# Attention's side work: full-width expert products, the inverse root on GpSimd, and a wider step limit for VectorE

## The chip, the cores and the metric

The kernel runs on one core of a Trainium2 chip. The metric is the device time of one execution in microseconds. A core has TensorE (PE, with its weight loads listed as PEld), VectorE (DVE), ScalarE (ACT), GpSimd (POOL) and SyncE (SP), which here only issues transfers. Each engine works off its own queue in order and waits on semaphores of the others.

## The reference, cut to what matters

Input is x of 8 images, 128 channels, 64 x 64 pixels, in float32. Layer 0 is a Mamba-like scan block with group norm. Layer 1 sees each image as 4096 tokens of 128 channels and adds an additive attention and a mixture of 64 experts:

```python
t = _to_tokens(x)
t = t + _L1_attn_ref(_ln_t(t), W1, b1, w2, b2)          # causal: weights exp(w2 . tanh(f_i + g_j + b1) + b2)
t = t + _L1_ffn_ref(_ln_t(t), gate_w, gate_b, weight1, weight2)

def _ln_t(v, eps=1e-5):                                  # layer norm over the channels
    return (v - mean) / sqrt(var + eps)

# in _L1_ffn_ref, for each image and each of 64 experts:
probs = softmax(logits over the tokens)                  # logits = x @ gate_w.T + gate_b
vals, idx = top_k(probs, 8)                              # each expert takes its 8 best tokens
pooled = sum over the 8 of vals * x[idx]                 # a 128-vector for each expert
# ... two small dense layers on pooled; the result, times vals, is added back to those 8 tokens
```

The change lies in two places of this: in the layer norm before the experts (the factor 1/sqrt(var + eps)) and in the product that makes `pooled`.

## The kernel before, in words

The kernel has two large stages. `mamba` works through 64 chunks of 512 tokens (the first 1.5 ms). `attend` then works through the causal attention of all eight images, and at its end the experts' dense layers and the output.

**The attention loop.** The score matrix of an image is cut into tiles of 128 keys by 512 queries; the diagonal ones are packed, so that there are 132 tiles for each image and 1056 in all. The loop `for i in range(-3, n + 3)` is a software pipeline over them. For each `i` it issues, in this order:

- `rounds` (L718): PE makes the numerators N of tile i and the denominators D of tile i+3, as products with 32 rows of weights, four of them side by side in the array. D and N have one set of PSUM banks each.
- `logarithms` (L728, L729): ACT takes the logarithm of D into a tile called `mix`, which frees D.
- `inverses` (L735): ACT takes one exponential over four planes of 512 columns: three inverse denominators and the weights exp(-score) of an earlier tile.
- `ratios` (L740): DVE multiplies N by the inverses, three operations of 128 x 512; each frees a bank of N.
- `weigh` (L766): PE multiplies the finished weights of tile i-3 with the tokens and adds into the bank `av`. At the end of a row of tiles `take` (L777) copies `av` to `sums` on DVE.
- `advance(("p", "next", "alone"), ...)`: side steps that issue PE work (below).
- `causal` (L746): a mask on GpSimd, for diagonal tiles.
- `advance(("v", "free", "end"), ...)`: side steps for DVE.
- `scores` (L753, L754): DVE adds two of the ratios, GpSimd adds the third (128 x 512 each) into the plane that `inverses` exponentiates next.

**The side steps.** What follows the attention (its normalisation, the second layer norm, the logits, the choice of eight tokens, the product for `pooled`) is written as generators in two lanes, `finishing` and `routing`. Each `yield` names a kind and a written cost for what comes next: "p" opens a group of PE work in the one PSUM bank `ms`, "next" goes on with it, "free" is the DVE step that empties the bank, "v" is DVE work, and "end" ends the lane's turn in this tile. `advance` takes steps from the lanes' fronts as long as their kinds fit and their written costs stay within a limit (the first step is always taken):

```python
if spent and spent + cost > room or kind in ("p", "alone") and holder:
    break
```

The limit for PE is 0.37 (0.6 in the last image while `more` holds). For DVE it is 1.4 while `more` holds, that is, while more than three generators are listed in the two lanes, and otherwise 0.8.

For each of the 64 groups of 512 tokens, `finish` normalises the attention's result (L842 on PE, L847 to L851 on DVE), then `route` runs `normalise` (L792 bn_stats, L795 bn_aggr, L796 adding epsilon into `rs`, L798 and L799 on ACT for the inverse root, L802 four scalings into `lnf`), transposes (L811, L813) and makes logits (L878, L887, L889). Once for each image `choose` picks the tokens (L931 to L979, with ACT's exponentials in L944), and for seven of the eight images goes through four groups of: transposing the weights (L1007, L1010) and the product for `pooled` (L1016 on PE, L1026 or L1028 on DVE).

**The product.** A column of 128 weights holds 64 experts for a token block of the first half and the same 64 experts for a block of the second half. L1016 multiplies each 64-column half with its own block of 128 tokens, into its own 64 partitions of the bank. In the records each float32 product counts as two MATMULs.

Of the kernel before, what the change touches and what calls it, by code (L numbers as in the profile page):

```python
# [10 lines left out]
AF = mybir.ActivationFunctionType  # L11
ALU = mybir.AluOpType
AX = mybir.AxisListType

P = 128
# [3 lines left out]
NE = 64  # L19
# [43 lines left out]
def fast_path(  # L63
# [24 lines left out]
    nc = tc.nc  # L88
# [4 lines left out]
    NQ = CH // P  # L93
# [9 lines left out]
    def fixed(name, *shape):  # L103
        return const.tile(list(shape), F32, name=name)
# [10 lines left out]
    gamma, beta, gateb = fixed("gamma", P, 1), fixed("beta", P, 1), fixed("gateb", P, 1)  # L115
    wuv, biasv, wcol = fixed("wuv", P, 2, P), fixed("biasv", P, 1), fixed("wcol", P, 1)
    back, shift, tiny = fixed("back", P, P + 1), fixed("shift", P, 1), fixed("tiny", P, 1)
    floor = fixed("floor", P, 1)
    gwide = fixed("gwide", P, 3 * NE)

    def halves(queue, t, src):
# [2 lines left out]
    def prepare(mw, bank):  # L124
# [90 lines left out]
        nc.vector.tensor_scalar(tiny, tiny, 1e-10, None, ALU.mult)  # L215
        nc.vector.memset(shift, -SHIFT)
        nc.vector.memset(floor, EPS)
        nc.vector.tensor_reduce(gsel, ident.rearrange("p (g c) -> p g c", c=GROUP), AX.X, ALU.add)
        nc.vector.tensor_scalar(
            gmean3, gsel.unsqueeze(2).to_broadcast([P, P // GROUP, GROUP]), 1.0 / GROUP, None, ALU.mult  # L220
# [437 lines left out]
    def attend(aw, small, ap, remaining):  # L658
# [18 lines left out]
        n = len(tiles)  # L677
        per, held = n // B, []
        U, V, tok, tt, lnf = {}, {}, {}, {}, {}
# [101 lines left out]
        def bank(name):  # L781
            return ap.tile([P, CH], F32, tag="ms", name=name)

        def normalise(n, src, dst):

            st = small.tile([P, NQ, 6], F32, tag="st", name=f"st{n}")
            mv = small.tile([P, NQ, 2], F32, tag="lmv", name=f"lmv{n}")
            rs = small.tile([P, NQ], F32, tag="rs", name=f"rs{n}")
            for q in range(NQ):
                if q:  # L790
                    yield "v", 0.2
                nc.vector.bn_stats(st[:, q, :], src[:, q, :])  # L792
            yield "v", 0.45
            for q in range(NQ):
                nc.vector.bn_aggr(mv[:, q, :], st[:, q, :])  # L795
            nc.vector.tensor_scalar(rs, mv[:, :, 1], EPS, None, ALU.add)  # L796
            yield "end", 0.0
            nc.scalar.activation(rs, rs, AF.Ln)  # L798
            nc.scalar.activation(rs, rs, AF.Exp, scale=-0.5)  # L799
            for q in range(NQ):  # L800
                yield "v", 0.26
                nc.vector.tensor_scalar(  # L802
                    dst[:, q, :], src[:, q, :], mv[:, q, 0:1], rs[:, q : q + 1], ALU.subtract, ALU.mult
                )
# [10 lines left out]
        def bring(b, g):  # L815


            n = f"{b}_{g}"
            c = b * NCH + g
            u = U[b, g] = aw.tile([P, 2, CH], F32, tag="U", bufs=4, name=f"U{n}")  # L820
            v = V[b, g] = aw.tile([P, 2, CH], F32, tag="V", bufs=NCH + 1, name=f"V{n}")
            queue = nc.gpsimd if c < 3 else nc.sync
            for ab, to, at in ((0, 0, 64), (0, 64, 0), (1, 0, 96), (1, 64, 32)):
                for which in range(2):
                    rows = slice(to + 32 * which, to + 32 * (which + 1))
                    queue.dma_start(u[rows, ab, :], uv_dram[c][0, at : at + 32, :])
                    queue.dma_start(v[rows, ab, :], uv_dram[c][1 + which, at : at + 32, :])
            t = tt[b, g] = aw.tile([P, NQ, P], F32, tag="tt", bufs=NCH, name=f"tt{n}")
            k = tok[b, g] = aw.tile([P, NQ, P], F32, tag="tok", bufs=NCH + 1, name=f"tok{n}")
            for r, dst in enumerate((t, k)):  # L830
                nc.sync.dma_start(dst.rearrange("p q c -> p (q c)"), k_dram[c][r])
# [59 lines left out]
        def choose(b):  # L891

            n = f"{b}"
# [86 lines left out]
            if final:  # L980
# [3 lines left out]
                for g, tag in enumerate(("D2", "N0", "av", "ms")):  # L984
# [4 lines left out]
                    mT = aw.tile([P, NQ, P], F32, tag="mT", bufs=2, name=f"mT{n}_{g}")  # L989
# [5 lines left out]
                acc = aw.tile([P, P], F32, tag="acc", name=f"acc{n}")  # L995
                nc.vector.tensor_copy(acc, total)
                pp = ap.tile([P, CH], F32, tag="N0", name=f"pp{n}")
# [4 lines left out]
            for g in range(NCH // 2):  # L1002
                for q in range(NQ):
                    yield "next" if q else "p", 0.14
                    if q == 0:
                        pm = bank(f"pm{n}_{g}").rearrange("p (q e) -> p q e", e=P)
                    nc.tensor.transpose(pm[:, q, :], w[:, 2 * g + q // 2, ts(q % 2, P)], ident)  # L1007
                yield "free", 0.6
                mT = aw.tile([P, NQ, P], F32, tag="mT", bufs=2, name=f"mT{n}_{g}")
                nc.vector.tensor_copy(mT, pm)  # L1010
                for q in range(NQ):
                    yield "next" if q else "p", 0.18
                    if q == 0:
                        pp = bank(f"pp{n}_{g}")
                    for h in range(2):
                        nc.tensor.matmul(  # L1016
                            pp[ts(h, NE), :P],
                            lhsT=mT[:, q, ts(h, NE)],
                            rhs=lnf[b, 2 * g + q // 2][:, 2 * h + q % 2, :],
                            start=q == 0,  # L1020
                            stop=q == NQ - 1,
                        )
                yield "free", 0.3
                if g == 0:
                    acc = aw.tile([P, P], F32, tag="acc", name=f"acc{n}")
                    nc.vector.tensor_copy(acc, pp[:, :P])  # L1026
                else:
                    nc.vector.tensor_tensor(acc, acc, pp[:, :P], ALU.add)  # L1028
            yield "p", 0.26
            pp = bank(f"pp{n}")  # L1030
            nc.tensor.matmul(pp[:, :NE], lhsT=acc, rhs=stack, start=True, stop=True)
# [46 lines left out]
        def biases():  # L1078

            wb1 = aw.tile([NE, NH * P], F32, tag="wb1", name="wb1")  # L1080
            nc.sync.dma_start(wb1, weight1[:, P, :])
            wb2 = aw.tile([NE, P], F32, tag="wb2", name="wb2")
            nc.sync.dma_start(wb2, weight2[:, NH * P, :])
            return wb1, wb2
# [231 lines left out]
        def upcoming(lane):  # L1316

            while lane:
                if id(lane[0]) not in waits:
                    waits[id(lane[0])] = next(lane[0], None)  # L1320
                if waits[id(lane[0])] is not None:
                    return waits[id(lane[0])]
                del waits[id(lane[0])]
                done.append(lane.pop(0))
            return None
# [5 lines left out]
        def advance(kinds, room):  # L1331

            spent = 0.0
            for lane in lanes:
                while (step := upcoming(lane)) is not None and step[0] in kinds:
                    kind, cost = step
                    if spent and spent + cost > room or kind in ("p", "alone") and holder:
                        break
                    spent += cost
                    waits[id(lane[0])] = next(lane[0], None)  # L1340
                    if kind == "p":
                        holder.append(lane)
                    if kind == "free":
                        holder.clear()
                    if kind == "end":
                        break
# [11 lines left out]
        for i in range(-3, n + 3):  # L1358
            if i == n - NQ * NCH:
                small_rows = biases()  # L1360
            cur = i if 0 <= i < n else None
            nxt = i + 3 if i + 3 < n else None
            inv = i + 2 if 0 <= i + 2 < n else None
            last = i - 1 if 0 <= i - 1 < n else None
            if 0 <= i < n:
                b, at = divmod(i, per)
                for more, g in begin.get(at, []):
                    if b + more < B:
                        bring(b + more, g)
            if i < n:  # L1370
                room(i + 1)
            for g in feed.get(i - (n - NQ * NCH + 2), []):
                next(supply[g], None)

            more = len(finishing) + len(routing) > 3
            rounds(cur, nxt)
            if nxt is not None:
                logarithms(i + 1, nxt)
            if inv is not None or last is not None:
                inverses(i, inv, last)  # L1380
            if cur is not None:
                ratios(cur)
            complete = [weigh(i - 3)] if i >= 3 else []
            advance(("p", "next", "alone"), 0.6 if more and i > n - per else 0.37)
            if i >= 2 and i - 2 < n:
                causal(i - 2)
            advance(("v", "free", "end"), 1.4 if more else 0.8)
            if cur is not None:
                scores(cur)
            for key in complete:  # L1390
                if key is not None:
                    take(*key)
# [648 lines left out]
```

## Time and profile before

| | |
|---|---|
| median of 3 runs | 5213.81 us (5211.79 to 5220.13) |
| the profiled execution's own time | 5218.64 us |
| its span, first to last instruction | 5216.9 us |
| busy share of the span: PE, ACT, DVE, POOL | 95%, 94%, 89%, 39% |
| attention loop (L728 first to last start) | from 1532.9 us to 5006.1 us |
| instructions of L798 and L799 on ACT | 64 each, mean 211 and 206 ns |
| MATMUL records of L1016 | 448, in 28 groups |

Times in the profile are microseconds from the start of the span unless marked ns. "Idle before" is the time an engine stood still just ahead of an instruction, and "<-" names what it waited for. Instructions of an engine overlap a little at their ends, so the start-to-start distance is the better price of one in a full queue.

### The profile page before, as it was taken

How to read it: one execution, taken by the hardware profiler on the slowest of the kernel's cores; microseconds unless marked ns; L12 is line 12 of the kernel's file. 1: busy time of each engine (PE TensorE's matmuls, PEld its weight loads, DVE VectorE, ACT ScalarE, POOL GpSimd, SP SyncE). 2: the span in 40 equal slices, each digit the busy share in tenths (PEclk: the TensorE clock that was granted, in tenths of full speed). 3: DMA queues.
4: the chain of work that ended last, by engine and by line, in shares of the span. 5: the costliest groups of instructions: out<-in, count | busy, mean ns of one | idle time of the engine just before them, and what ended most of it. 6: DMA issues, size and time to landing. Idle time of an engine off the chain costs nothing. (4 is left out here: it accounts for less than half of the span.)

```text
span 5216.9 us, 80416 instructions
## 1 busy us (share of the span) xinstructions
PE 4956.4 (95%) x27566; PEld 2263.8 (43%) x27566; DVE 4643.8 (89%) x8307; ACT 4892.6 (94%) x5750; POOL 2044.1 (39%) x1888
## 2 busy tenths in 40 slices
PE   7899999999879999999999999999999999999987
PEld 2344444444334434444444444444444444444443
DVE  8999999999939989999999999989999999998962
ACT  7899999999969999999999999999999999999962
POOL 3444344444424444344334434444434443443421
PEclk9999999999979999999999999999999999999998
DMA  3244444444451011101111101110111110111058
GB/s 98 90 143 150 150 152 157 158 158 156 138 192 33 25 43 34 37 21 51 38 29 39 56 25 44 34 38 25 48 38 29 42 54 25 44 28 57 21 175 352
DMA packets 203365, 420.74 MB, mean 81 GB/s; under 512 B 52211, under 2 KB 52867, under 8 KB 192963
## 3 DMA queue, kind: packets, MB, share of 16 engines
q1 hardware_dynamic: 192146, 394.39, 23.6%
q0 software_dynamic: 10240, 20.73, 1.1%
q8 instruction: 220, 3.60, 0.3%
q14 instruction: 199, 1.62, 0.1%
q10 hardware_dynamic: 560, 0.39, 0.0%
HBM read 291.45 MB, written 123.47 MB: 80 GB/s over the span
## 5 line engine op out<-in xcount | busy, mean ns | idle before, releaser
L740 DVE TENSOR_TENSOR mix<-mix,N 128x512 f32<-128x512 f32 x3168 | 2046.4, 684 | 285.6 <-PE N L718 186.7
L718 PE MATMUL D<-U,V 32*128 32x512 f32 (+3 forms) x9216 | 2117.7, 578 | 84.8 <-ACT mix L728 54.2
L754 POOL TENSOR_TENSOR mix<-mix 128x512 f32<-128x512 f32 x1056 | 1347.1, 1276 | 2080.9 <-DVE mix L753 1569.1
L718 PE MATMUL N<-U,V 32*128 32x512 f32 (+3 forms) x9216 | 2124.1, 577 | 0.0
L735 ACT ACTIVATE mix<-mix 128x2048 f32<-128x2048 f32 (+1 forms) x1059 | 2042.2, 1928 | 11.8 <-POOL mix L754 8.1
L718 PEld LDWEIGHTS D<-U,V 32*128 32x128 f32 x9216 | 842.7, 184 | 817.7 <-ACT mix L728 359.9
L766 PE MATMUL av<-mix,tok 128*128 128x512 f32 (+3 forms) x2304 | 1189.1, 605 | 8.4 <-DVE sums L777 5.3
L728 ACT ACTIVATE mix<-D 128x1024 f32<-128x1024 f32 x1056 | 1096.7, 1039 | 35.2 <-PE N L718 27.2
L718 PEld LDWEIGHTS N<-U,V 32*128 32x128 f32 x9216 | 843.6, 184 | 28.3 <-DVE mix L740 10.7
L753 DVE TENSOR_TENSOR mix<-mix 128x512 f32<-128x512 f32 x1056 | 724.6, 686 | 15.9
L766 PEld LDWEIGHTS av<-mix,tok 128*128 128x128 f32 x2304 | 350.8, 188 | 739.5 <-issue 646.3
L729 ACT ACTIVATE mix<-D 128x512 f32<-128x512 f32 x1056 | 646.8, 612 | 0.0
L397 POOL TENSOR_TENSOR hc<-hs,rep 128x1024 f32<-128x1024 f32 (+1 forms) x256 | 512.4, 2021 | 272.7 <-issue 174.0
L388 DVE TENSOR_TENSOR_SCAN hs<-da,hs,db 128x512 f32<-128x512 f32 x336 | 412.3, 1270 | 8.7 <-ACT da L375 3.5
L405 PE MATMUL py<-hc,ident 128*128 128x512 f32 x768 | 351.6, 594 | 0.0
L375 ACT ACTIVATE da<-dt,aneg 128x512 f32<-128x512 f32 x384 | 255.8, 691 | 40.5 <-DVE hs L388 39.0
L268 PE MATMUL px<-xt,wtap 128*128 128x512 f32 x512 | 274.7, 664 | 6.9 <-DVE wtap L137 6.9
L405 PEld LDWEIGHTS py<-hc,ident 128*128 128x128 f32 x768 | 147.5, 192 | 189.1 <-issue 187.6
L379 DVE TENSOR_TENSOR db<-dx,rep 128x1024 f32<-128x1024 f32 x192 | 229.0, 1219 | 0.0
L304 POOL DMA_DIRECT2D bc_dram<-bc x128 | 68.8, 542 | 367.5 <-ACT bc L302 367.5
L268 PEld LDWEIGHTS px<-xt,wtap 128*128 128x128 f32 x512 | 97.7, 201 | 150.3 <-issue 143.4
L279 PE MATMUL pz<-xt,wgate 128*128 128x512 f32 x256 | 127.1, 619 | 27.9 <-DVE y L361 23.5
(280 smaller groups left out, 5085.3 us busy)
## 6 DMA issues: line engine op xcount, KB each, us to landing
rep<-bc_dram SPq DMA_DIRECT2D x64, 1536.0 KB, 7.5
uv_dram<-uv SPq DMA_DIRECT2D x64, 768.0 KB, 9.4
w<-in_L_ffn_weight_dram SPq DMA_DIRECT2D x128, 256.0 KB, 5.4
U<-uv_dram SPq DMA_DIRECT2D x488, 64.0 KB, 2.0
V<-uv_dram SPq DMA_DIRECT2D x488, 64.0 KB, 2.0
xr<-in_x_dram SPq DMA_DIRECT2D x64, 256.0 KB, 8.0
k_dram<-tt SPq DMA_DIRECT2D x64, 256.0 KB, 7.8
k_dram<-tok SPq DMA_DIRECT2D x64, 256.0 KB, 9.5
```

Source lines behind the costliest of these rows:

```text
L268: nc.tensor.matmul(px, lhsT=wtap[:, tap, ts(h, P)], rhs=ch[c]["x"][:, ds(tap, CH)], start=tap == 0, stop=tap == 1,)
L388: nc.vector.tensor_tensor_scan(hs[:, h, :], ch[c].pop(("da", n, h)), db[:, h, :], first, ALU.mult, ALU.add)
L397: nc.gpsimd.tensor_tensor(hc[:, h, :], hs, ch[c]["rep"][:, 1, n, :].unsqueeze(1).to_broadcast(list(hs.shape)), ALU.mult)
L405: nc.tensor.matmul(py, lhsT=ident, rhs=ch[c]["hc", n][:, h, :], start=False, stop=n == NR - 1)
L718: nc.tensor.matmul(dst, lhsT=left, rhs=right, start=first, stop=final)
L728: nc.scalar.activation(x[:, 0:2, :], d01, AF.Ln)
L729: nc.scalar.activation(x[:, 2, :], d2, AF.Ln)
L735: nc.scalar.activation(mix[k][:, planes, :], mix[k][:, planes, :], AF.Exp, scale=-1.0)
L740: nc.vector.tensor_tensor(r[:, g, :], r[:, g, :], n[g], ALU.mult)
L753: nc.vector.tensor_tensor(r[:, 1, :], r[:, 1, :], r[:, 2, :], ALU.add)
L754: nc.gpsimd.tensor_tensor(mix[k + 1][:, 3, :], r[:, 0, :], r[:, 1, :], ALU.add)
L766: nc.tensor.matmul(av[0][:, q : q + cols], lhsT=tok[b, jb // NQ][:, jb % NQ, :], rhs=mix[t + 1][:, 3, at : at + cols], start=first and jb ...
```

## The change

Four edits, all for the attention stage:

1. `normalise` no longer takes ACT's logarithm and exponential of `rs` (128 x 4). GpSimd raises `rs` to the power -0.5 with one `tensor_tensor`, whose second input is a new constant `power`, filled once by DVE in the preparation.
2. The product for `pooled` takes all 128 columns of weights at once against two token blocks (256 columns), for each of the four steps of a group. Half of the result, each half of the experts with the other's tokens, isn't used. The written cost of a step is 0.36 instead of 0.18.
3. The sum into `acc` takes its two 64-partition parts with two DVE operations instead of one. Its written cost is 0.5 instead of 0.3.
4. The DVE limit of `advance` outside `more` is 1.05 instead of 0.8.

```diff
-    floor = fixed("floor", P, 1)
+    floor, power = fixed("floor", P, 1), fixed("power", P, NQ)
...
+        nc.vector.memset(power, -0.5)
...
             nc.vector.tensor_scalar(rs, mv[:, :, 1], EPS, None, ALU.add)
             yield "end", 0.0
-            nc.scalar.activation(rs, rs, AF.Ln)
-            nc.scalar.activation(rs, rs, AF.Exp, scale=-0.5)
+            nc.gpsimd.tensor_tensor(rs, rs, power, ALU.pow)
             for q in range(NQ):
                 yield "v", 0.26
...
                 for q in range(NQ):
-                    yield "next" if q else "p", 0.18
+                    yield "next" if q else "p", 0.36
                     if q == 0:
-                        pp = bank(f"pp{n}_{g}")
-                    for h in range(2):
-                        nc.tensor.matmul(
-                            pp[ts(h, NE), :P],
-                            lhsT=mT[:, q, ts(h, NE)],
-                            rhs=lnf[b, 2 * g + q // 2][:, 2 * h + q % 2, :],
-                            start=q == 0,
-                            stop=q == NQ - 1,
-                        )
-                yield "free", 0.3
+                        pp = bank(f"pp{n}_{g}")[:, : 2 * P]
+                    nc.tensor.matmul(
+                        pp,
+                        lhsT=mT[:, q, :],
+                        rhs=lnf[b, 2 * g + q // 2].rearrange("p (h k) c -> p k h c", h=2)[:, q % 2],
+                        start=q == 0,
+                        stop=q == NQ - 1,
+                    )
+                yield "free", 0.5
                 if g == 0:
                     acc = aw.tile([P, P], F32, tag="acc", name=f"acc{n}")
-                    nc.vector.tensor_copy(acc, pp[:, :P])
-                else:
-                    nc.vector.tensor_tensor(acc, acc, pp[:, :P], ALU.add)
+                for h in range(2):
+                    to, mine = acc[ts(h, NE), :], pp[ts(h, NE), ts(h, P)]
+                    if g == 0:
+                        nc.vector.tensor_copy(to, mine)
+                    else:
+                        nc.vector.tensor_tensor(to, to, mine, ALU.add)
...
-            advance(("v", "free", "end"), 1.4 if more else 0.8)
+            advance(("v", "free", "end"), 1.4 if more else 1.05)
```

## The prediction

> **What bounds the kernel now.** I read the busy shares first, then the busy times by stretch, to see whether one engine fills the attention loop. The chain that ended last reaches back only 15 us, to the output, and says nothing on this loop.
>
> ```profile
> PE 4956.4 (95%) x27566; PEld 2263.8 (43%) x27566; DVE 4643.8 (89%) x8307; ACT 4892.6 (94%) x5750; POOL 2044.1 (39%) x1888
> ```
> ```profile
> 2800.00:3600.00 800.00, 780.50 (x5222) 361.69 (x5222) 730.44 (x1416) 791.81 (x770) 324.49 (x302) 1.00 0.12 36
> ```
>
> The columns of the second are the stretch, its length and the busy time of PE, PEld, DVE, ACT and POOL. In 800 us of the loop ACT is busy for 99%, PE for 98%, DVE for 91%. So no engine has much room, and a saving on one counts only as far as the next allows. The measure for that is the tile's period, the distance from one start of L728 to the next, in ACT's order of time:
>
> ```profile
> 1707.89 1.02 ACT L728 ACTIVATE mix<-D 128x1024 f32<-128x1024 f32 x1
> ...
> 1709.28 1.92 ACT L735 ACTIVATE mix<-mix 128x2048 f32<-128x2048 f32 x1
> 1711.08 0.21 ACT L798 ACTIVATE rsf<-rsf 128x4 f32<-128x4 f32 x1
> 1711.33 0.21 ACT L799 ACTIVATE rsf<-rsf 128x4 f32<-128x4 f32 x1
> 1711.44 1.01 ACT L728 ACTIVATE mix<-D 128x1024 f32<-128x1024 f32 x1
> ```
> ```profile
> 2114.35 1.02 ACT L728 ACTIVATE mix<-D 128x1024 f32<-128x1024 f32 x1
> 2117.93 1.02 ACT L728 ACTIVATE mix<-D 128x1024 f32<-128x1024 f32 x1 [0.26 <-PE N L718]
> 2121.50 1.02 ACT L728 ACTIVATE mix<-D 128x1024 f32<-128x1024 f32 x1 [0.26 <-PE N L718]
> ```
>
> The first tile, with L798 and L799, took 3.55 us; the second view's two, with the products of L1016, 3.58 and 3.57, and there ACT waited for PE. I took all starts of L728 and sorted the tiles by their side work. Without any: 3.197 (ACT alone repeats in 3.18). With L798/L799: 3.703 on average over 61. With 4, 8, 12 records of L1016: 3.358 (4 tiles), 3.565 (48), 3.784 (4). With two records of L878, 0.215 us of PE: 3.206. With four transposes of L1007, 0.43 us of PE: 3.407 to 3.458 (4 tiles, mean 3.427).
>
> The third view is DVE around a `normalise`:
>
> ```profile
> 3499.33 0.48 DVE L887 TENSOR_SCALAR m<-pl,gateb 128x256 f32<-128x256 f32 x1
> 3499.85 0.43 DVE L889 MAX8 cand<-m 128x8 f32<-128x256 f32 x1
> 3500.19 0.66 DVE L792 BATCH_NORM_STATS2 stf<-tt 128x6 f32<-128x128 f32 x3
> 3500.77 0.68 DVE L753 TENSOR_TENSOR mix<-mix 128x512 f32<-128x512 f32 x1
> 3501.36 1.88 DVE L740 TENSOR_TENSOR mix<-mix,N 128x512 f32<-128x512 f32 x3
> 3503.15 0.29 DVE L792 BATCH_NORM_STATS2 stf<-tt 128x6 f32<-128x128 f32 x1
> 3503.36 0.36 DVE L795 BATCH_NORM_AGGREGATE lmvf<-stf 128x2 f32<-128x6 f32 x4
> 3503.76 0.17 DVE L796 TENSOR_SCALAR rsf<-lmvf 128x4 f32<-128x4 f32 x1
> 3503.84 0.68 DVE L753 TENSOR_TENSOR mix<-mix 128x512 f32<-128x512 f32 x1
> 3504.44 1.88 DVE L740 TENSOR_TENSOR mix<-mix,N 128x512 f32<-128x512 f32 x3
> 3506.23 1.11 DVE L802 TENSOR_SCALAR lnf<-tt,lmvf,rsf 128x128 f32<-128x128 f32 x4
> 3507.25 0.69 DVE L753 TENSOR_TENSOR mix<-mix 128x512 f32<-128x512 f32 x1
> ```
>
> From 3499.33 on DVE isn't idle once (no bracket of idle time stands behind a line): **here DVE bounds, not ACT.** Its tile of L798 lasted 3.80 us, 0.25 more than the 3.555 of the 32 undisturbed ones, because the late L753 makes L754 and so L735 late. This decides my forecast.
>
> **ScalarE's logarithm and exponential go.** 64 tiles of 3.703 against 3.197 are 32.4 us. Of it 64 x (3.555 - 3.18) = 24 is ACT's own work; the rest is DVE's lateness, which stays.
>
> **What DVE does with it.** From the trace's starts, an operation of 128 x 512 costs DVE 0.600 in a full queue; four make 2.40, so a period of 3.18 leaves 0.78 for side steps. Start to start: L887 with L889 0.86, one L792 0.195, L795 with L796 0.48, one L802 0.255, L847 to L851 0.975, one copy of 128 x 512 0.60. How much lateness is harmless shows in tiles with nothing on ACT: 0.24 us was followed by a period of 3.18, 0.42 by 3.39. I take 0.25.
>
> Playing `advance` with the old costs gives every tile's steps; its 48, 4 and 4 tiles of L1016 are those of the trace. The same with the new costs and limit gives, for the 64 `normalise`:
> - 20 as in the view above (three tiles with 1.46, 0.68, 1.02 us) and about 28 with 1.05, 1.07, 1.02: at 0.8 the four L792 (0.8) filled a tile and L802 (0.26 each) fell into 3 + 1; at 1.05 one L792 joins L889 and all four L802 stand together. Both sum to some 3.15 against 3 x 0.78 = 2.34, so 0.8 is left over, and past 0.25 some 0.55 us is lost. 48 x 0.55 = 26.
> - 7 with a `finish` between (1.17, 1.07, 0.98, 1.02 against 3.12): 1.1 over, 0.85 lost, 6 us.
> - 7 beside L1033 fit, and two or three meet the copy of L777 (0.6): 2 us.
>
> Together 34 against the 32.4 that go: **+2 us**. ScalarE's saving is real, but DVE needs about the same time in the same tiles.
>
> **The power on GpSimd.** No row has it. The nearest are a MEMSET of the same 128 x 4 (107 ns) and a TENSOR_TENSOR of 128 x 512 (1276 ns), so I take about 0.4 us, between them, with both ends kept; a gain below nothing is excluded, since nothing waits for GpSimd's speed here. GpSimd runs it behind the last L754 and `causal`; behind it stands this tile's L754, and behind that ACT's L735 and PE's L766. But L754 must wait for L753 anyhow, which starts 0.08 after L796 and whose end reaches GpSimd 0.85 after its start (3500.77 to 3501.62): 0.8 us are free, and some 0.5 more until L735 comes. DVE's L802 follows a tile later. Cost: 0 up to 1.3 us; each further us costs 64.
>
> **The products.** Two steps a tile become one: 56 tiles become 112. The trace starts pairs of old records, both halves at once, 0.109 us apart. A record of 512 columns takes 0.427 in a row, so one of 256 takes 0.213 and a step 0.43, as much as the four transposes: 3.427. Old excess: 48 x 0.368 + 4 x 0.587 + 4 x 0.161 = 20.3. New: 112 x 0.23 = 25.8. **+5.5 us.**
> On this the Trainium skill, "TensorEngine Tiling", says two things. Its Overview (Theoretical Speedup) gives halves of up to 64 columns up to twice the speed, which speaks against the change; the pairs 0.109 us apart agree, and by that alone each old pair of steps, 0.44 us, would become 0.86, 56 x 0.42 = 24 us more. Its Tiling Modes (Key Properties) say that a change of mode drains the array, which speaks for it. In the rows, 3.358, 3.565 and 3.784 rise by 0.21 for each 4 records and leave some 0.13 a tile for such a switch, 56 x 0.13 = 7 us, which is within the 20.3 above.
>
> **The sum into `acc`.** One operation of 0.205 more (start to start of L1028), 28 times: 5.7 us of DVE, each in a tile with 0.25 to spare. Nothing; if that cover is gone, 5.7.
>
> **The rest of the limit.** The steps of `choose` come two tiles earlier and denser. Two tiles of 3.37 and 3.45 stand after them in each image now, with no other side work than DVE's: that is DVE's lateness again, 0.4 us, and I allow as much once more in seven images, 3 us, from 0 to 6. And 69 more tiles hold some PE work, which costs 0.01 to 0.05 each (3.206 to 3.247 against 3.197): 2 us. **+5 us**, from 0 to 8. The lanes empty in the same 13 rounds after the loop, and nothing in the last image's choice is changed. `power`'s fill in the preparation is one small DVE operation, at most 0.1 us.
>
> **Sum:** 2 + 5.5 + 5 = +12.5 us on the profiled execution's 5218.64, which stands 4.8 over the median of 5213.81. Against the median: **5226**.
>
> **Rivals.**
> *DVE's lateness is harmless* (faster). The allowance of 0.25 comes from few tiles, some with PE work in them. Were it 0.8, the 34 us of new loss vanish: -32.4 + 5.5 + 5 = -22, so 5192. It decides from an allowance of 0.5, at which 48 routes lose 0.3 each, 14 us, and the sum is about -7. For it: one tile with 0.24 cost nothing, and L754 costs ACT only 8.1 us in 11 waits. Against it: DVE never idles in the view above.
> *The power is slow* (slower yet). At 2 us, (2 - 1.3) x 64 = 45 more: 5271. For it: power isn't one pass of arithmetic. Against it: only 4 columns.
> *The limit doesn't do what it says.* Only 508 of 1062 rounds are outside `more`. If the denser steps were evened out by the next tiles, only products remain: about 5214 to 5220, no change.
>
> **How the numbers follow.** A measurement of this kernel tells some 0.2%, 10 us, from no change: 5203.4 to 5224.2. My forecast (5217 to 5240) has 0.60, the harmless lateness 0.16, the slow power 0.12, no change by evening out 0.12. From these: faster 0.15, same 0.27, slower 0.58. The range reaches from half of the first rival's way to part of the slow power's: 5202 to 5252.
>
> **What would show it.** Right: no L798 and no idle ACT made up for it but ACT waiting more for PE's N and for L754, and DVE without idle time over three tiles of each route; periods near 3.43 in 112 tiles of L1016; a power of under 1 us. Wrong: routes' tiles at 3.18 to 3.25 with four L802 in them, or L1016's tiles at 3.2 (then it is faster), or L754 waiting for the power.

## The result, and the profile after

The changed kernel takes 5239.19 us (median of 5 runs, 5237.46 to 5240.78) against 5213.81 us: a ratio of 1.0048, 95% interval 1.0037 to 1.0059. It is **25 us slower**, where 12 us were forecast. The profiled execution's span grew by 20.6 us, from 5216.9 to 5237.5, and 19.8 of these lie between the first and the last tile of the attention loop. It grew by less than the median, because the profiled execution of before lay 4.8 us over its median.

Below, lines from L218 to L797 of before stand one line further down, because of the line that fills `power`: L728 is now L729, L735 is L736, L740 is L741, the scores on DVE are L754 and on GpSimd L755, the copy of the sums is L778. The power is L799, the scalings are still L802, the products are L1015.

First a row of before: ACT's exponential, with its instructions, busy time, mean ns, and the idle time ahead of it with what ended it:

```profile
L735 ACT ACTIVATE mix<-mix 128x2048 f32<-128x2048 f32 (+1 forms) x1059 | 2042.2, 1928 | 11.8 <-POOL mix L754 8.1
```

After the change, the page's busy row, the busy times in the same 800 us (PE, PEld, DVE, ACT, POOL), and three rows of the groups:

```profile
PE 4970.2 (95%) x27342; PEld 2296.3 (44%) x27342; DVE 4666.8 (89%) x8336; ACT 4890.7 (93%) x5622; POOL 2133.9 (41%) x1952
```
```profile
2800.00:3600.00 800.00, 781.18 (x5133) 367.74 (x5132) 730.38 (x1405) 787.28 (x739) 341.39 (x314) 1.00 0.13 37
```
```profile
L736 ACT ACTIVATE mix<-mix 128x2048 f32<-128x2048 f32 (+1 forms) x1059 | 2037.9, 1924 | 46.3 <-POOL mix L755 42.8
...
L799 POOL TENSOR_TENSOR rsf<-rsf,power 128x4 f32<-128x4 f32 x64 | 88.6, 1384 | 86.3 <-DVE rsf L797 84.6 <-PE N L719 1.7
...
L1015 PE MATMUL pp<-lnf,mT 128*128 128x256 f32 x224 | 66.7, 379 | 0.0
```

PE and DVE are as busy as before in these 800 us; ACT lost 4.5 us. Its exponential L736 now waits 42.8 us for GpSimd's scores, where L735 waited 8.1. And one power on 128 x 4 elements takes 1.384 us, longer than GpSimd's whole addition of 128 x 512 (1.276).

One `normalise` shows the way from the one to the other. First GpSimd, then DVE, then ACT, over the same stretch:

```profile
2317.41 1.28 POOL L755 TENSOR_TENSOR mix<-mix 128x512 f32<-128x512 f32 x1 [2.65 <-PE N L719]
...
2320.21 1.38 POOL L799 TENSOR_TENSOR rsf<-rsf,power 128x4 f32<-128x4 f32 x1 [1.04 <-DVE rsf L797]
2321.57 1.27 POOL L755 TENSOR_TENSOR mix<-mix 128x512 f32<-128x512 f32 x1
```
```profile
2318.97 0.67 DVE L793 BATCH_NORM_STATS2 stf<-tt 128x6 f32<-128x128 f32 x3
2319.56 0.36 DVE L796 BATCH_NORM_AGGREGATE lmvf<-stf 128x2 f32<-128x6 f32 x4
2319.95 0.17 DVE L797 TENSOR_SCALAR rsf<-lmvf 128x4 f32<-128x4 f32 x1
2320.03 0.69 DVE L754 TENSOR_TENSOR mix<-mix 128x512 f32<-128x512 f32 x1
2320.63 1.88 DVE L741 TENSOR_TENSOR mix<-mix,N 128x512 f32<-128x512 f32 x3
2322.43 1.27 DVE L802 TENSOR_SCALAR lnf<-tt,lmvf,rsf 128x128 f32<-128x128 f32 x4
```
```profile
2318.82 1.94 ACT L736 ACTIVATE mix<-mix 128x2048 f32<-128x2048 f32 x1
2320.62 1.05 ACT L729 ACTIVATE mix<-D 128x1024 f32<-128x1024 f32 x1
2321.53 0.64 ACT L730 ACTIVATE mix<-D 128x512 f32<-128x512 f32 x1
2322.87 1.91 ACT L736 ACTIVATE mix<-mix 128x2048 f32<-128x2048 f32 x1 [0.71 <-POOL mix L755]
2324.69 1.01 ACT L729 ACTIVATE mix<-D 128x1024 f32<-128x1024 f32 x1
```

The power waits for `rs` until 2320.21. DVE's part of the scores ends at 2320.72, so GpSimd's part could have begun shortly after, but it stands behind the power and begins at 2321.57. It ends at 2322.84, and at 2322.87 ACT, idle for 0.71 us, goes on. The tile from 2320.62 to 2324.69 lasts 4.07 us. ACT is rid of 0.37 us in one tile and stands still for about twice that in the next.

The products did what was forecast. Four tiles of L1015, by ACT's starts, where the old ones took 3.58 and 3.57:

```profile
2129.38 1.03 ACT L729 ACTIVATE mix<-D 128x1024 f32<-128x1024 f32 x1
2132.80 1.02 ACT L729 ACTIVATE mix<-D 128x1024 f32<-128x1024 f32 x1
2136.27 1.02 ACT L729 ACTIVATE mix<-D 128x1024 f32<-128x1024 f32 x1 [0.16 <-PE N L719]
2139.70 1.03 ACT L729 ACTIVATE mix<-D 128x1024 f32<-128x1024 f32 x1
2143.15 1.03 ACT L729 ACTIVATE mix<-D 128x1024 f32<-128x1024 f32 x1
```

To see all tiles at once I took ACT's starts from each trace and sorted the tiles as the steps fall: those around a `normalise` (the tile before the root's, the root's own, three after), those with products, those of `choose` with its transposes, and the rest. The root's own tile is the one in which epsilon is added (L796 of before). The table has the time over 3.18 us a tile, in us, for before, after and the experiments that follow; in brackets are the root's own tiles and those right after.

| kernel | around `normalise` (root; next) | products | `choose` | rest |
|---|---|---|---|---|
| before | 39.2 (32.6; 0.2) | 21.6 | 26.1 | 31.2 |
| after | 59.9 (7.9; 44.4) | 27.3 | 30.9 | 19.9 |
| power alone | 37.2 (14.2; 15.7) | 21.6 | 26.1 | 28.1 |
| products alone | 40.0 (29.0; 0.3) | 27.2 | 25.8 | 38.2 |
| limit alone | 47.3 (28.6; 1.1) | 22.3 | 29.0 | 25.2 |
| multiplication for power | 38.1 (7.8; 9.5) | 27.5 | 30.6 | 27.2 |
| power behind scores | 31.6 (8.6; 7.2) | 27.4 | 30.6 | 25.0 |

The root's tiles fell by 24.7 us and the next ones rose by 44.2. Small differences in the last column tell nothing: the rest holds the loop's first ten tiles, and these cost 10.1 us before and 7.1 with the power alone, although both kernels have the same steps there (5.7 after the change).

### The profile page after: what moved, and what is told of

The parts are those of the page before. It is cut to its first block, busy times and chain, and to the rows that moved or that the text cites. A ratio compares the mean times of both kernels' runs of the same rounds, so it can differ in the third digit from the quotient of the medians.

```text
span 5237.5 us, 80096 instructions
## 1 busy us (share of the span) xinstructions
PE 4970.2 (95%) x27342; PEld 2296.3 (44%) x27342; DVE 4666.8 (89%) x8336; ACT 4890.7 (93%) x5622; POOL 2133.9 (41%) x1952
## 5 line engine op out<-in xcount | busy, mean ns | idle before, releaser
L741 DVE TENSOR_TENSOR mix<-mix,N 128x512 f32<-128x512 f32 x3168 | 2041.1, 684 | 277.6 <-PE N L719 186.1
L755 POOL TENSOR_TENSOR mix<-mix 128x512 f32<-128x512 f32 x1056 | 1348.6, 1277 | 1932.7 <-DVE mix L754 1557.6
L736 ACT ACTIVATE mix<-mix 128x2048 f32<-128x2048 f32 (+1 forms) x1059 | 2037.9, 1924 | 46.3 <-POOL mix L755 42.8
L729 ACT ACTIVATE mix<-D 128x1024 f32<-128x1024 f32 x1056 | 1093.9, 1036 | 27.1 <-PE N L719 9.4
L754 DVE TENSOR_TENSOR mix<-mix 128x512 f32<-128x512 f32 x1056 | 725.5, 687 | 19.9
L730 ACT ACTIVATE mix<-D 128x512 f32<-128x512 f32 x1056 | 644.3, 610 | 0.0
L280 PE MATMUL pz<-xt,wgate 128*128 128x512 f32 x256 | 129.0, 627 | 28.1 <-DVE y L362 23.6
```

The costliest lines, as they stand in the source:

```text
L729: nc.scalar.activation(x[:, 0:2, :], d01, AF.Ln)
L730: nc.scalar.activation(x[:, 2, :], d2, AF.Ln)
L736: nc.scalar.activation(mix[k][:, planes, :], mix[k][:, planes, :], AF.Exp, scale=-1.0)
L741: nc.vector.tensor_tensor(r[:, g, :], r[:, g, :], n[g], ALU.mult)
L754: nc.vector.tensor_tensor(r[:, 1, :], r[:, 1, :], r[:, 2, :], ALU.add)
L755: nc.gpsimd.tensor_tensor(mix[k + 1][:, 3, :], r[:, 0, :], r[:, 1, :], ALU.add)
```

## The experiments

Two theories stood after this. **P**: the power's own time, in front of the scores in GpSimd's queue, makes ACT wait. **L**: the limit packs DVE's steps, and its lateness is what ACT waits for, as the prediction had it. All ratios are to the kernel before, with 95% intervals; 0.001 is 5.2 us.

**The parts alone.**

```diff
-            nc.scalar.activation(rs, rs, AF.Ln)
-            nc.scalar.activation(rs, rs, AF.Exp, scale=-0.5)
+            nc.gpsimd.tensor_tensor(rs, rs, power, ALU.pow)
```

> The kernel before with the power on GpSimd alone (old products, old sum, limit 0.8). Theory P (the power itself, 1.38 us against 0.8 us that L753 hides, makes the next exponential of ACT wait): the tiles of the root lose 0.37 us of ACT (64 x 0.37 = 24 us gained), the tiles after them gain 0.5 to 0.7 us (32 to 45 us lost): 8 to 20 us slower than before, ACT waits for GpSimd's scores by over 25 us in all. Theory L (the limit of 1.05 packs VectorE's steps, and its lateness is what ACT waits for): without that limit about 20 us faster than before, ACT's wait for GpSimd at or below 10 us.

Measured: 5209.39 us, ratio 0.9992 (0.9983 to 1.0001), some 4 us faster or nothing. Neither theory's number. In the table ACT gains 18 us in the root's tiles and loses 15.5 in the next; L736 waits 17.6 us for GpSimd.

```diff
-                    for h in range(2):
-                        nc.tensor.matmul(pp[ts(h, NE), :P], lhsT=mT[:, q, ts(h, NE)], ...)
+                    nc.tensor.matmul(pp, lhsT=mT[:, q, :], ...)      # 256 columns; with the two-part sum and its costs
```

> The kernel before with the full-width products and the two-part sum alone. Both theories: 112 tiles of about 3.42 us instead of 56 of 3.565, 5 to 7 us slower than before.

Measured: 5227.73 us, ratio 1.0027 (1.0018 to 1.0036), 14 us slower: twice the forecast. The tiles of the products rose by 5.6 us as expected, and the rest by 7. There 12 tiles of 4.05 us or a little more appear, which the kernel before doesn't have. One of them, DVE first and then PE:

```profile
2323.45 0.48 DVE L887 TENSOR_SCALAR m<-pl,gateb 128x256 f32<-128x256 f32 x1
2323.96 0.43 DVE L889 MAX8 cand<-m 128x8 f32<-128x256 f32 x1
2324.30 0.67 DVE L753 TENSOR_TENSOR mix<-mix 128x512 f32<-128x512 f32 x1
2324.90 0.68 DVE L777 COPY sums<-av 128x512 f32<-128x512 f32 x1
```
```profile
2325.73 1.53 PE L766 MATMUL av<-mix,tok 128*128 128x512 f32 x4 [0.44 <-DVE sums L777]
```

The new pace of the products moves every later step, and the step of the logits (L887, L889) falls into the tile in which DVE copies the sums. The copy ends late, PE waits 0.44 us for the bank `av`, in a tile whose L766 has four records instead of two, and then ACT waits for PE.

```diff
-            advance(("v", "free", "end"), 1.4 if more else 0.8)
+            advance(("v", "free", "end"), 1.4 if more else 1.05)
```

> The kernel before with the limit of 1.05 alone. Theory P: the limit costs little, 0 to 5 us slower. Theory L: VectorE's three full tiles in a row cost here too, 8 to 12 us slower, with the tiles after the root at 3.4 us or more.

Measured: 5220.86 us, ratio 1.0013 (1.0004 to 1.0022), 7 us slower, between the two. The tiles after the root stay at 3.197; the loss is one tile further (3.315 instead of 3.223) and before the root. The rest gains 6 us, 2.6 of them in the first ten tiles.

The three ratios add up to some 17 us, not 25. Something in them works together.

**The power's duration.** The same operands, place, order and waits, but a multiplication instead of the power:

```diff
-            nc.gpsimd.tensor_tensor(rs, rs, power, ALU.pow)
+            nc.gpsimd.tensor_tensor(rs, rs, power, ALU.mult)
```

> The changed kernel with a multiplication in the place of the power on GpSimd: same operands, place, order and waits, another value of the inverse root. Theory P: the multiplication takes under 0.4 us, the tiles after the root fall from 3.885 to about 3.2 to 3.35 us, and the kernel is 35 to 44 us faster than the changed one, 10 to 20 us faster than before. Theory L: the steps of VectorE are the same, so it stays within 5 us of the changed kernel, 20 to 25 us slower than before.

Measured: 5221.38 us, ratio 1.0011 (1.0002 to 1.0021): 18 us under the changed kernel, 6 or 7 over before. DVE's steps are the same, and the scores behind the multiplication aren't held up by it: they start some 0.85 us after DVE's, as before the change, and with the power it is 1.54. So 18 us are the power's duration, which P has, but less than its 35 to 44: DVE's lateness then shows in the two tiles after (3.331 and 3.360), which L has. Even the multiplication takes 0.565 us:

```profile
L799 POOL TENSOR_TENSOR rsf<-rsf,power 128x4 f32<-128x4 f32 x64 | 36.2, 565 | 88.0 <-DVE rsf L797 86.3 <-PE N L719 1.7
```

**The power's place.** GpSimd is busy for 41% only. The power is issued behind this tile's scores, and its scalings one tile later:

```diff
-            nc.gpsimd.tensor_tensor(rs, rs, power, ALU.pow)
+            behind.append(lambda: nc.gpsimd.tensor_tensor(rs, rs, power, ALU.pow))
+            yield "end", 0.0
...
             if cur is not None:
                 scores(cur)
+            while behind:
+                behind.pop(0)()
```

> The changed kernel with the power issued behind this tile's scores on GpSimd, and its four scalings one tile later. Theory P (the power holds up the scores that are queued behind it): ACT's wait for GpSimd's scores falls from 43 us to under 10 us, the tiles after the root from 3.885 to about 3.3, and the kernel comes to about 5218 us, 18 to 25 us under the changed one. Theory L (VectorE's steps are late by themselves): no more than 5 us under the changed one.

> The kernel before with the power alone, issued behind this tile's scores, its scalings one tile later; old products, limit 0.8. Theory P: the 32 us that the root's tiles cost over the others are gained but for some 8 us of VectorE's lateness: 18 to 25 us faster than before. Theory L: VectorE needs the time anyhow, so no better than the power alone in its first place, 3 to 8 us faster than before.

Measured in the changed kernel: 5214.66 us, ratio 1.0001 (0.9992 to 1.0010), 24 us under the changed kernel. L736 waits 8.9 us for GpSimd, about as before the change. **Moving the power behind the scores, with its scalings a tile later, brings 24 us, about all that was lost.** Of these, 18 went with the power's duration alone, as the multiplication showed with nothing moved. The other 6 or 7 can't be the power's wait: the multiplication holds up no scores either, and yet the tiles around `normalise` cost 38.1 us there and 31.6 here. It is likely DVE, whose four scalings now come a tile later; no run moves these alone. One row for ACT, and GpSimd in that kernel:

```profile
L736 ACT ACTIVATE mix<-mix 128x2048 f32<-128x2048 f32 (+1 forms) x1059 | 2036.3, 1923 | 17.7 <-POOL mix L755 8.9
```
```profile
2269.91 1.28 POOL L755 TENSOR_TENSOR mix<-mix 128x512 f32<-128x512 f32 x1 [1.80 <-DVE mix L754]
2271.14 1.03 POOL L799 TENSOR_TENSOR rsf<-rsf,power 128x4 f32<-128x4 f32 x1
2272.43 1.28 POOL L755 TENSOR_TENSOR mix<-mix 128x512 f32<-128x512 f32 x1 [0.26 <-DVE mix L754]
```

The power runs in time that GpSimd spent idle, and the next scores wait for DVE and not for it. It also takes 1.02 us instead of 1.38, of which more below.

In the kernel before, with nothing else changed: 5206.53 us, ratio 0.9983 (0.9974 to 0.9992), 9 us faster, where P had 18 to 25 and L 3 to 8. The tiles around `normalise` fell from 39.2 to 18.8 us over 3.18, as P has it, but the rest rose from 31.2 to 40.7. Of that, 6.0 us stand in tiles in which DVE copies the sums and in those right after: with the scalings all later steps move, and the copy of the transposes (L813) and the step of the logits now meet it too. In 35 of the 64 tiles of the copy DVE has more than 0.5 us of side steps, before it was 24.

**Undoing a part.**

```diff
-            advance(("v", "free", "end"), 1.4 if more else 1.05)      # the changed kernel
+            advance(("v", "free", "end"), 1.4 if more else 0.8)
```

> The changed kernel with the limit back at 0.8. If the parts add up as they did alone (power -4 us, products +14 us): about 10 us slower than before, 15 us under the changed kernel, with tiles of 4.05 us where the logits' step and the copy of the sums meet. If the limit of 1.05 keeps these meetings apart and is worth it: no faster than the changed kernel.

Measured: 5225.22 us, ratio 1.0018 (1.0009 to 1.0027), 9 us slower than before: power and products simply add, and 12 tiles of 4.05 us are there too, as expected. The tiles after the root take 17.0 us over 3.18 instead of 44.4.

> The changed kernel with the old products and the one-part sum. The products' own price is 6 us in the changed kernel by its tiles (27.3 against 21.6 us over 3.18), so 5 to 8 us under the changed kernel, about 18 us slower than before: then power and limit together cost much more than the sum of each alone (-4 and +7 us). If the parts add up: about 3 us slower than before.

Measured (old products and one-part sum in the changed kernel): 5237.91 us, ratio 1.0045 (1.0031 to 1.0059), 24 us slower than before. So **power and limit together cost 24 us, and alone -4 and +7**. The tiles after the root take 44.3 us, as in the changed kernel. That undoing the products brings 5 to 8 us did not show: their tiles fall by 5.0 us, but the tiles around `normalise` and the rest take more than that back. The intervals of the two kernels, 6 or 7 us to either side, don't exclude a gain of this size.

**The most that the root can give.** The kernel before without L798 and L799 and with nothing in their place (the scaling takes the variance itself):

> The kernel before without the logarithm and the exponential of the inverse root, and with nothing in their place (the scaling takes the variance itself): the most that any move of them can gain. If ScalarE's time in these tiles is free for the taking: 24 us or more faster than before. If VectorE's lateness stands behind it, as in the prediction: 10 to 16 us faster.

Measured: 5200.16 us, ratio 0.9971 (0.9960 to 0.9981), 15 us faster. ACT's 24 us are not free for the taking: the root's tiles still take 3.398 us on average, without any root. In 22 of them, of 3.41 to 3.48 us, DVE is late: the exponential starts within 0.06 us of the end of GpSimd's scores, and these start about 0.85 us after DVE's. Seven more, of about 4.1 us, stand right behind a copy of the sums. The others take 3.18 to 3.36.

**The copy kept clear.** The meetings of L777 can be avoided by giving DVE no side steps in those 64 tiles:

```diff
-            advance(("v", "free", "end"), 1.4 if more else 0.8)
+            if not any(complete):
+                advance(("v", "free", "end"), 1.4 if more else 0.8)
```

> The kernel before with the full-width products and the two-part sum, and no side steps for VectorE in the 64 tiles in which it copies the sums. If the products' own price is 6 us and the other 8 of the 14 us that they cost alone come from steps that were shifted onto the copy: 4 to 8 us slower than before, no tile of 4.05 us. If the products cost it by themselves: 12 to 15 us slower.

> The kernel before with no side steps for VectorE in the 64 tiles in which it copies the sums, and nothing else. If the products' own price is 6 us (so that the run with both, which came out at no difference, holds a gain and a loss): 5 to 10 us faster than before. If the products cost nothing once the copy is clear: no difference.

Measured: 5216.43 us, ratio 1.0000 (0.9991 to 1.0009) with the products, and 5209.80 us, 0.9989 (0.9980 to 0.9999) without. With the products that is faster than the 4 to 8 us slower that were expected, because to keep the copy clear is worth some 4 to 6 us by itself. The difference of the two, 0.0011 or 6 us, is the products' own price, though two intervals of 0.0009 leave it uncertain by itself; that their tiles cost 27.1 against 20.1 us, and that no tile of 4.05 us is left, agrees with it. So of the 14 us that they cost alone about 6 are their own and about 8 come from steps that they push onto the copy.

**A version that beats both.** The power behind the scores, the copy kept clear, old products, limit 0.8:

> The power behind the scores (old products, limit 0.8), and no side steps for VectorE in the 64 tiles in which it copies the sums. If those meetings hold TensorE up: 5 to 8 us under the same kernel with them, 13 to 17 us faster than before. If they do not matter: 9 us faster than before, as there.

Measured: 5196.34 us, ratio 0.9960 (0.9947 to 0.9974): **21 us faster than before and 43 us under the changed kernel.** That is more than the 13 to 17 us that were expected. The tiles around `normalise` take 17.3 us over 3.18 instead of 39.2, and those of the copy and right after it, without the loop's first ten tiles, 12.2 instead of 22.1. The median is even 4 us below that of the kernel without any root, whose side steps still meet the copy; by the intervals the two could be equal.

## Why the prediction was right or wrong

The forecast was 5226 (+12.5), within 5202 to 5252, slower at 0.58. It is slower, by 25 us. Term by term:

- **The root leaves ACT.** 24 us were counted as ACT's own work; the root's tiles fell by 24.7. Right, and the kernel without any root shows that at the old limit only 15 of it can be kept.
- **DVE's lateness.** The mechanism was right, and the size nearly so. 34 us were put on the 64 `normalise`, for a net +2. The kernel with the multiplication shows it by itself, since it has the same DVE steps and holds up no scores: all tiles around `normalise` take 38.1 us over 3.18 there, against 39.2 before, a net -1.
- **The power, the step that failed.** It was taken as 0.4 us and as free up to 1.3. Its duration is 1.384, just outside the upper row of the two between which it was put. By that price the 0.084 over would cost 5 us; it cost 18, or 0.28 us a tile. So less was free than 1.3.

  The view of one `normalise` above shows why. The power could start only 0.18 after DVE's L754, so that of the 0.85 after which GpSimd could go on with the scores 0.67 were free, not 0.8. And of the 0.5 us that were added until the exponential needs the scores nothing was left: without the power they would have run from about 2320.88 to 2322.15, by an estimate from these rows, and ACT's L730 ends at 2322.17. Before the change, the exponential never started right behind these scores (within 0.06 us of their end); with the multiplication and the limit of 1.05 it did in 36 of 63 cases, with the power in all 63.

  The limit puts three of the four L793 into DVE's tile of the root in 35 of the 64 cases, and one in 21, so the scores are late by that already, and the power comes on top. At the limit of 0.8 it is none in 42 cases and one in 21. With the power in front, ACT waited over 0.15 us for the scores in 21 of the tiles after the root at 0.8 (8.7 us in the power alone), and in 55 at 1.05 (33.6 us). This is why power and limit together cost 21 us more than alone. The prediction had this packing, and its third view already shows a late L753 that makes L735 late, but it gave the power its slack in a sum of its own.
- **The products.** 3.427 a tile and +5.5 us were forecast; 3.424 and +5.7 were measured. The four transposes were the right row. The old excess was added up wrongly (48 x 0.368 + 4 x 0.587 + 4 x 0.161 is 20.7, not 20.3), which makes the forecast's own term 5.1; the difference is small. The prediction drew on the Trainium skill's "TensorEngine Tiling" for the speed of 64-column halves and for the drain at a change of mode: the runs show what the two come to, 6 us over 112 tiles for giving the halves up. Neither is measured by itself; the 0.13 us a tile for the change of mode is the difference of 3.565 and 3.427, two kinds of tiles of about the same PE time. That the written cost also shifts all later steps was not thought of: about 8 us, when the products stand alone.
- **The rest of the limit.** +5 us were allowed, for `choose` 3 of them. `choose` with its transposes cost 4.8 more. The rest of the tiles gained 11.3, not forecast. Of these, 4.4 lie in the loop's first ten tiles, which differ by 3 us between kernels with the same steps there, so they say nothing of the change. Another 6.0 lie in tiles of the copy and right after it, but that is no gain for the copy: all tiles of this kind, without the first ten, cost 22.1 us before and 30.7 after, since now steps of `choose` meet it.
- **The rivals.** The slow power was the one that came, with the mechanism it had, at 1.38 us and not at 2. "L754 waiting for the power" was named as a sign of being wrong, and it came; "a power of under 1 us" was named as a sign of being right, and it didn't. Harmless lateness is refuted by the kernel without a root (15 us, not 24) and by the multiplication (tiles of 3.33 to 3.36 after the root). That the limit evens out is refuted too: alone it costs 7 us.

So the power's term was too small by 22 us around `normalise` (59.9 with it, 38.1 with the multiplication), DVE's too large by 3, and 11 us of the rest went unseen. With these the forecast of +12.5 becomes the +20 of the two profiled executions. That the sum came within 13 us of the measured 25 is partly luck: an unseen gain, part of it from those first ten tiles, offset half of the power's loss.

What stays open: why undoing the products in the changed kernel brings no gain that can be measured. By the profile their 5 us move into other tiles (1.6 of them into the first ten); no run shows which step takes the others, and the intervals are too wide to say that nothing was gained. Also open is how much of the 24 us belongs to the scalings' later tile.

## What to carry to other kernels

An operation moved to an idle engine is not free because the engine is idle: ask what is queued behind it there, and who waits for that. Here the power's duration cost 18 us in front of the scores, and behind them ACT waited for GpSimd no longer than before the change. In a loop whose PE, ACT and DVE are all over 90% busy, cost edits together and not one after the other, since they draw on the same slack; and a change to the pace of side steps moves every later one, so look for what they will now meet.

## What the runs showed of the hardware that was not expected

A GpSimd `tensor_tensor` on 128 x 4 elements depends on what DVE does beside it. These rows are the power and the multiplication where DVE has stopped, in the drain behind the loop:

```profile
5046.62 1.02 POOL L799 TENSOR_TENSOR rsf<-rsf,power 128x4 f32<-128x4 f32 x1 [6.89 <-DVE rsf L797]
```
```profile
5029.87 0.20 POOL L799 TENSOR_TENSOR rsf<-rsf,power 128x4 f32<-128x4 f32 x1 [8.55 <-DVE rsf L797]
```

Alone, the power takes 1.02 us and the multiplication 0.20; in the loop they take 1.38 and 0.57: there 63 of the 64 start beside DVE's addition of two operands from SBUF (0.69 us). The surcharge is about the same for both, 0.37 us. In the view of 2320.21 DVE's next operation starts 0.42 us after the power did, so this fits a GpSimd operation that stands still until DVE's addition is nearly over; no run starts the two at another distance. Behind the scores, where DVE's long operations read one operand from PSUM, the power took 1.02 again (mean 1.019 over 64). The Trainium skill's "GPSIMD Engine Reference" (Specifications) says that the two engines share their SBUF interfaces and contend when a DVE instruction has two SBUF inputs; these runs agree and put a size on it for this case. Four columns of power cost 0.82 us more than four of multiplication, by which a column costs some 0.2 us more, an estimate.
